# Cross-attention with a routed expert layer: expert weights kept on chip and copied by register, the last group routed like all others, sets of 9, 4 and 3 groups

## The chip, the cores and the metric

The kernel runs on one core of a Trainium2 chip. The metric is the time of one execution on the device in microseconds (us); lower is better. The core has a tensor engine (PE; its weight loads are listed as PEld), a vector engine (DVE), a scalar engine (ACT), a GpSimd engine (POOL) and SyncE (SP), which here only issues transfers. Each engine works through its own instructions in order, and semaphores tie the engines together.

## The reference

64 sequences of 128 tokens, 128 features each. First cross-attention to a context of 77 rows, then a mixture of 8 experts of which each token takes two, and a shared expert for all tokens:

```
x = x + xattn(layernorm(x), ctx)          # 16 heads of 64, softmax, output projection, bias
x2 = layernorm(x); logits = x2 @ router_w.T
idx = top_k(softmax(logits), 2)           # gate[t, e] = logits[t, e] for the two chosen, else 0
for e in range(8):
    h = silu(x2 @ w1[e].T) * (x2 @ w3[e].T)          # 176 hidden
    moe += gate[:, e:e+1] * (h @ w2[e].T)
moe += (silu(x2 @ sw1.T) * (x2 @ sw3.T)) @ sw2.T     # shared expert
x = x + moe
```

Everything is float32.

## The kernel before

**Groups, units, steps.** The 64 sequences are 16 groups of 4 (`G`), 512 tokens each. Attention runs over 128 units (one sequence, half of the heads); a hand-written plan (`at(step, ...)`) hangs all other work on 256 steps, two for each unit, so 16 for each group. Each engine's order is the order in which the program is written out: a last loop ties every instruction to the one before it on its engine.

**Routing.** While group g+1 is in attention, a `Router` normalises group g, transposes it, computes the logits (L514), chooses two experts for each token (`choose`, `choose_second`, small DVE operations), and in `place` (L554 to L599) counts with PE and DVE which row of a DRAM buffer each token goes to. `send` (L604) scatters the rows with 8 indirect DMAs that POOL issues, one for each sequence and choice. The shared expert follows, and `park` (L633) writes the sum to DRAM.

**Sets and blocks.** Groups are collected in sets (`SETS`, 7, 5 and 3). When a set's last group is placed, `tables` (L692) makes on DVE the table of blocks: which 128 rows belong to which expert. A `Quad` is four blocks of 128 rows; sets of 7, 5 and 3 groups have 16, 12 and 8 quads, always worked in full. `Quad.load` (L748) reads from the tables into SP registers and has SP issue, for each block, one DMA for its rows (`xb`, L757) and one for its expert's weights (`w`, L765, 312 KB from DRAM). Then `transpose` (PE L771, ACT L773), `first` and `rest` (PE L778, ACT tanh L465 and L477, DVE L467 to L482), `down` (PE L790 and L791, the destination rows `to` on DVE L793, the scaling `y` on ACT L798) and `answer`: four indirect DMAs on POOL (L802), which scatter the results to DRAM. `Combine` reads a group's parked rows (L821) and its answers (L822, 512 KB), adds them on DVE (L829, two additions) and has SP store the result (L833).

**What runs where.** The quads of the first two sets are spread over attention steps. Their p (the step of `transpose`) goes from `st.ready` to shortly before the next set is ready: 16 quads over steps 127 to 203, 12 over 207 to 251.

**The ending.** After attention, `ending` works through 17 jobs in an order of its own: the 8 quads of the last set, the shared expert of the last group, and the last group itself, which is not routed: class `Dense` passes all its 512 tokens through each of the 8 experts (PE L655, L669, L670) and adds each result with the gate as a factor (DVE L672). Quads and dense jobs alternate; the last three jobs are dense. In iteration k the program writes `first` of job k, `transpose` of job k+1, `rest` of job k, then `down` and `answer` of job k-1. The five combines of the set before the last and the three of the last set have their transfers issued by POOL; their additions are written two iterations behind their loads. Buffers: `y` has 2, `xb` 4, the weights `w` 12, `ya` 3.

**Last values.** `values_of_last` (L424) takes its staging tile from the same single buffer ("c") as the comparisons of `tables`.

Of the kernel before, what the change touches and what calls it, by code (L numbers as in the profile page):

```python
# [31 lines left out]
G = 4  # L32
NG = B // G

SETS = (7, 5, 3)
# [13 lines left out]
NHR = 3  # L49
# [3 lines left out]
NOWHERE = 1e6  # L53
# [5 lines left out]
def xattn_moe_kernel(  # L59
# [32 lines left out]
    def weights_of(engine, w, q, n, name):  # L92

        to = ffn.tile([128, WALL], F32, tag="w", name=f"{name}_{q}", bufs=3 * QUAD)
        to = to[:, : 4 * n].rearrange("p (m d) -> p m d", d=n)
        engine.dma_start(out=to, in_=w[:, 4 * q : 4 * (q + 1), :])
        return to
# [40 lines left out]
    wsh_sb = const.tile([128, WALL], F32, name="wsh_sb")  # L138
    nc.scalar.dma_start(out=bo_sb, in_=b_out.rearrange("(o d) -> o d", o=1).broadcast_to([128, D]))
    nc.sync.dma_start(out=rw_sb, in_=rwT)  # L140
    nc.sync.dma_start(out=wsh_sb, in_=wsh)

# [25 lines left out]
    dest = const.tile([128, most, 2 * G], F32, name="dest")  # L168
    spare = const.tile([128, nb], F32, name="spare")
# [8 lines left out]
    def more_constants():  # L178
        for e in range(E):
            nc.gpsimd.memset(rank[:, :, e : e + 1], float(E - e))  # L180
        nc.gpsimd.memset(upto, 0.0)
        for e in range(E):
            nc.gpsimd.memset(upto[:, e, : e + 1], 1.0)
            nc.gpsimd.memset(first_row[:, e : e + 1], float(e * rows))
        iota(block_no, [[1, nb]], 0, 0)
        iota(block_row, [[128, nb]], 0, 0)
        nc.gpsimd.memset(ones, 1.0)
        nc.gpsimd.affine_select(before, ones, [[1, 128]], ALU.is_gt, 0.0, base=0, channel_multiplier=-1)
        iota(dest, [[2 * T, most], [1, 2 * G]], 0, 2 * G)
        iota(spare, [[128, nb]], most * 2 * T, 1)  # L190
        for h in hrs:
            nc.gpsimd.memset(h, 0.0)
        nc.gpsimd.memset(nobody, 0.0)
        nc.gpsimd.memset(nobody[:, D : D + 1], NOWHERE)
        for to in sent:
            nc.sync.dma_start(out=to[E * rows :, :], in_=nobody)
# [99 lines left out]
    class Attention:  # L296
# [15 lines left out]
        def keys(self, p, i):  # L312

            if i == 0:
                self.kx[p] = grp.tile([D, NH, KP], F32, tag="kx", name=f"kx_{self.g}_{p}")
# [169 lines left out]
    class Router:  # L485


        def __init__(self, g, st, x1):
            self.g, self.st, self.x1 = g, st, x1
            self.j = g - st.start if st else None  # L490
# [63 lines left out]
        def place(self):  # L554
# [24 lines left out]
            for src, to, by in ((at, pos, 1.0), (self.lg, self.pay[:, :, :, D + 1].rearrange("p c b -> p c b"), 0.5)):  # L579
# [9 lines left out]
            nc.vector.tensor_copy(  # L589
                self.pay[:, :, :, D], dest[:, j, :].rearrange("p (c b) -> p c b", c=2)  # L590
# [44 lines left out]
    class Dense(Router):  # L635


        def __init__(self, g, st, x1):
            super().__init__(g, st, x1)
            self.w, self.he, self.hre = {}, {}, {}  # L640

        def gates(self):

            sel = self.t3("place")
            nc.vector.tensor_tensor(sel, self.oh[:, 0], self.oh[:, 1], ALU.add)
            self.gate = self.t3("grest")
            nc.vector.scalar_tensor_tensor(self.gate, self.lg, 0.5, sel, ALU.mult, ALU.mult)

        def load(self, e):
            self.w[e] = ffn.tile([128, WALL], F32, tag="w", name=f"w_d{e}", bufs=3 * QUAD)  # L650
            nc.sync.dma_start(out=self.w[e], in_=wx[e * 128 : (e + 1) * 128, :])

        def up_of(self, e):
            def up(to, c, m):
                nc.tensor.matmul(to[:m], self.w[e][:, c : c + m], self.x2T, start=True, stop=True)  # L655

            return up

        def first(self, e):
            self.he[e] = gated(f"d{e}", self.up_of(e))  # L660

        def rest(self, e):
            self.hre[e] = gated_rest(f"d{e}", self.up_of(e))

        def down(self, e):
            py = bank(f"pd_{e}")
            for b in range(G):
                ts = slice(b * NQ, (b + 1) * NQ)
                nc.tensor.matmul(py[:, ts], self.he[e][:, ts], self.w[e][:, W2F:W2R], start=True, stop=False)  # L669
                nc.tensor.matmul(py[:, ts], self.hre[e][:, ts], self.w[e][:, W2R:], start=False, stop=True)  # L670
            for b in range(G):
                nc.vector.scalar_tensor_tensor(  # L672
                    self.x1[:, b, :],
                    py[:, b * NQ : (b + 1) * NQ],
                    self.gate[:, b, e : e + 1],
                    self.x1[:, b, :],
                    ALU.mult,
                    ALU.add,
                )
                if e == E - 1:  # L680
                    nc.sync.dma_start(out=out[self.g * G + b], in_=self.x1[:, b, :])

    def values(a, most):
        return nc.values_load_multi_w_load_instructions(
            a,
            engines=[mybir.EngineType.SP],
# [5 lines left out]
    def tables(st):  # L692
# [47 lines left out]
        nc.vector.tensor_scalar(st.w_row, ex, float(E - 1), 128.0, ALU.min, ALU.mult)  # L740

    class Quad:
# [5 lines left out]
        def load(self):  # L748
            st = self.st
            self.w = []  # L750
            self.xb = ffn.tile([128, QUAD, DW], F32, tag="xb", name=f"xb_{self.name}", bufs=4)
            first = slice(QUAD * self.q, QUAD * (self.q + 1))
            froms = values(st.from_row[0:1, first], E * rows)
            wrows = values(st.w_row[0:1, first], (E - 1) * 128)
            for j in range(QUAD):
                w = ffn.tile([128, WALL], F32, tag="w", name=f"w_{self.name}_{j}", bufs=3 * QUAD)
# [8 lines left out]
                nc.sync.dma_start(out=w, in_=wx[bass.ds(wrows[j], 128), :])  # L765
                self.w.append(w)
# [19 lines left out]
        def down(self):  # L786
            py = bank(f"pq_{self.name}")
            for j in range(QUAD):
# [5 lines left out]
                self.to, self.xb[:, :, D], spare[:, QUAD * self.q : QUAD * (self.q + 1)], ALU.min  # L794
# [17 lines left out]
    class Combine:  # L812
# [5 lines left out]
        def load(self):  # L818
# [5 lines left out]
                in_=answers[st.i][j * 2 * T : (j + 1) * 2 * T, :].rearrange("(p k) d -> p k d", p=128),  # L824
# [75 lines left out]
    def route(g, step, *args):  # L900
        if g not in routers:
            st = next((s for s in sets if s.start <= g < s.start + s.n), None)
            routers[g] = (Router if st else Dense)(g, st, atts[g].x1)
# [10 lines left out]
    assert g == NG - 1  # L914
# [3 lines left out]
    for st in sets:  # L918
        for g in range(st.start, st.start + st.n):
            p = 16 * (g + 1)  # L920
            routing(g, p, (7, "place"), (11, "shared_up"), (12, "shared_rest"), (14, "shared_down"), (17, "park"))
            for k in range(4):
                for c in range(2):
                    at(p + 8 + k, lambda g=g, c=c, b=k: routers[g].send(c, b))
        at(p + 9, lambda st=st: tables(st))

        st.ready = p + 15
    end = 16 * NG

    for st, after in zip(sets, sets[1:]):  # L930
        until = after.ready - 4
        for q in range(st.quads):
            quad = Quad(st, q)
            p = st.ready + (until - st.ready) * q // (st.quads - 1)
            at(p - 3, quad.load)
            at(p, quad.transpose)
# [12 lines left out]
    class Job:  # L949


        def __init__(self, of=None, **steps):
            self.steps = {k: getattr(of, k) for k in ("load", "transpose", "first", "rest", "down") if hasattr(of, k)}
            self.steps.update(steps)
            if of is not None:
                self.steps["answer"] = lambda: [of.answer(j) for j in range(QUAD)]

        def do(self, step):
            self.steps.get(step, lambda: None)()

    def last(step, *args):
        return lambda: route(NG - 1, step, *args)

    before_last, last_set = sets[-2:]
    blocks = [Job(Quad(last_set, q)) for q in range(last_set.quads)]
    experts = [
        Job(load=last("load", e), first=last("first", e), rest=last("rest", e), down=last("down", e)) for e in range(E)
    ]
    shared = Job(first=last("shared_up"), rest=last("shared_rest"), down=last("shared_down"))
    jobs = blocks[:3] + [shared]  # L970
    for q, e in zip(blocks[3:], experts):
        jobs += [q, e]
    jobs += experts[len(blocks) - 3 :]

    ahead_of = {0: ["stats"], 1: ["normed"], 2: ["transpose", "logits"], 3: ["choose"], 4: ["choose_second", "gates"]}

    def finish(c, k):

        for n, step in ((0, c.load), (2, c.add), (2, c.store)):
            combining.setdefault(k + n, []).append(step)  # L980

    combining = {}
    for j in range(before_last.n):
        finish(Combine(before_last, j, nc.gpsimd), 2 + j)
    done = jobs.index(blocks[-1])
    for j in range(last_set.n):
        finish(Combine(last_set, j, nc.gpsimd), done + 2 + j)

    def ending():
        for k in range(max(len(jobs) + 2, max(combining) + 1)):  # L990
            job = jobs[k] if k < len(jobs) else Job()
            for step in ahead_of.get(k, ()):
                route(NG - 1, step)
            if k + 2 < len(jobs):
                jobs[k + 2].do("load")
            for step in combining.get(k, ()):
                step()
            job.do("first")
            if k + 1 < len(jobs):
                jobs[k + 1].do("transpose")  # L1000
            job.do("rest")
            if 0 < k <= len(jobs):
                jobs[k - 1].do("down")
                jobs[k - 1].do("answer")

    at(end - 3, lambda: jobs[0].do("load"))
    at(end - 2, lambda: jobs[1].do("load"))
    at(end - 1, lambda: jobs[0].do("transpose"))
# [132 lines left out]
```

## Time and profile before

| | |
|---|---|
| time, three runs | 1002.66 us median (1001.15 to 1005.33) |
| the profiled execution | 1007.26 us, of which 1005.6 us are the span from its first to its last instruction |
| busy share of the span | PE 96%, DVE 68%, ACT 61%, POOL 51% |
| granted PE clock, mean | 0.98 |
| DMA queues | 130.6 MB, mean 130 GB/s |
| weights `w` from DRAM | 144 loads of 312 KB for blocks, 8 for the dense jobs |
| indirect DMAs on POOL | 120 of `send`, 144 of `answer` |

Times within the profile are microseconds from the span's start, single durations often in nanoseconds (ns). A line of a timeline has the start, the duration, the engine, the source line, the operation, the written and read tiles, a count, and in brackets how long the engine had been idle and what ended that. A line of the windows view has, for a stretch of time, the busy time of PE, PEld, DVE, ACT and POOL with the number of instructions, then the granted clock, the share of the DMA engines and GB/s. A line of the chain of waits has the start, the duration and what the end of the program then depended on.

### The profile page before, as it was taken

The page shows a single profiled execution, that of the slowest core. Times are in us where ns is not written, and L with a number is a line of the kernel's source. Part 1 is how long each engine was busy: PE and PEld are TensorE (multiplying, and loading weights), DVE is VectorE, ACT ScalarE, POOL GpSimd, SP SyncE. Part 2 cuts the span into 40 slices and gives each one's busy share as a digit, 9 for nine tenths or more (in the row PEclk, how much of TensorE's full clock was granted, in tenths as well). Part 3 has the DMA queues.
Part 4 walks back from the last instruction along what each step waited for, and adds up shares of the span by engine and source line. Part 5 has one row for each costly group of instructions (what it writes and reads, how often), then busy time and mean ns, then how long its engine had stood idle before and what let it go on. Part 6 is the DMA issues. An engine that isn't in the chain of part 4 may idle for free.

```text
span 1005.6 us, 19274 instructions
## 1 busy us (share of the span) xinstructions
PE 960.8 (96%) x6219; PEld 791.8 (79%) x6219; DVE 682.9 (68%) x1758; ACT 612.9 (61%) x1345; POOL 512.9 (51%) x693
## 2 busy tenths in 40 slices
PE   7999999999999989999999999999999899898896
PEld 5887877777778858888788888887878788787684
DVE  4566776676666765857567666687668856665876
ACT  4776767666766655566666676665756656544341
POOL 3245363645455442574645648465465474663532
PEclk9999999999999999999999999999999999898997
DMA  5222112212211125544533454336568653267954
GB/s 174 69 63 74 45 43 74 74 31 64 71 57 58 56 85 162 159 133 129 172 117 105 129 178 144 106 112 195 187 205 266 213 161 119 71 193 230 340 183 147
DMA packets 100165, 130.62 MB, mean 130 GB/s; under 512 B 13408, under 2 KB 64352, under 8 KB 100064
## 3 DMA queue, kind: packets, MB, share of 16 engines
q1 hardware_dynamic: 84496, 96.27, 32.0%
q0 software_dynamic: 10240, 23.73, 6.8%
q10 hardware_dynamic: 5328, 9.37, 2.5%
q8 instruction: 50, 0.82, 0.4%
q14 instruction: 51, 0.42, 0.2%
HBM read 93.59 MB, written 35.74 MB: 129 GB/s over the span
## 4 chain that ended last, share of the span: by engine, by line
PE 75%; DVE 10%; ACT 7%; DMA 3%; issue 3%; POOL 1%; SPq 1%; DVEq 0%; ACTq 0%; POOLq 0%
PE py L415 13%; PE ps L336 11%; PE pk L319 10%; PE pv L388 8%; PE p L778 6%; PE pa L405 6%; PE pq L790 3%; PE pq L791 3%; PE p_s L615 2%; PE pn L425 2%; PE ph L778 2%; ACT pay L276 2%; ACT vo L393 1%; DVE sm L358 1%; PE pf L628 1%
## 5 line engine op out<-in xcount | busy, mean ns | idle before, releaser
L319 PEld LDWEIGHTS pk<-cT,wkq_sb 96*128 96x128 f32 x1024 | 158.2, 189 | 69.5 <-issue 45.2
L326 ACT COPY kx<-pk 128x308 f32<-128x308 f32 x256 | 105.2, 416 | 157.4 <-PE pk L319 152.3
L802 POOL DMA_INDIRECT answers<-y,to x144 | 141.2, 981 | 104.6 <-ACT y L798 47.1
L319 PE MATMUL pk<-cT,wkq_sb 96*128 96x154 f32 x1024 | 175.1, 294 | 0.7 <-DVE wkq_sb L237 0.7
L336 PE MATMUL ps<-kx,xgT 128*128 128x308 f32 x512 | 158.7, 431 | 5.3 <-DVE sc L347 5.3
L415 PEld LDWEIGHTS py<-vo,aT 128*128 128x128 f32 x1280 | 154.6, 194 | 11.2 <-ACT vo L393 1.8
L415 PE MATMUL py<-vo,aT 128*128 128x128 f32 x1280 | 155.2, 277 | 1.6 <-ACT vo L393 1.6
L604 POOL DMA_INDIRECT sent<-pay,row x120 | 118.3, 986 | 61.6 <-DVE part L594 30.7
L393 ACT COPY vo<-pv 64x512 f32<-64x512 f32 x256 | 147.2, 575 | 2.1 <-ACT vn L433 0.4
L368 POOL TENSOR_TENSOR at<-sc,ri 128x512 f32<-128x512 f32 x64 | 67.4, 1053 | 154.8 <-DVE ri L360 118.2
L351 ACT ACTIVATE sc<-sc,rs_a 128x616 f32<-128x616 f32 x128 | 104.9, 819 | 50.5 <-DVE sc L347 41.0
L358 DVE TENSOR_REDUCE sm<-sc 128x8 f32<-128x616 f32 x128 | 101.2, 790 | 44.9 <-ACT sc L351 44.1
L388 PE MATMUL pv<-wvo_sb,cM 96*128 96x512 f32 x256 | 131.0, 593 | 0.2 <-DVE x L416 0.2
L366 POOL TENSOR_TENSOR at<-sc,ri 128x256 f32<-128x256 f32 x128 | 76.2, 618 | 104.4 <-DVE ri L360 53.1
L408 ACT COPY aT<-pa 128x512 f32<-128x512 f32 (+1 forms) x256 | 96.4, 430 | 42.5 <-PE pa L405 35.7
L336 PEld LDWEIGHTS ps<-kx,xgT 128*128 128x128 f32 x512 | 89.1, 191 | 30.2 <-DVE sc L347 6.0
L345 DVE TENSOR_REDUCE mx<-ps 128x8 f32<-128x616 f32 x128 | 98.7, 771 | 19.7 <-PE ps L336 18.4
L347 DVE TENSOR_TENSOR sc<-ps,mx 128x616 f32<-128x616 f32 x128 | 102.4, 800 | 12.9 <-DVE mx L345 1.0
L405 PE MATMUL pa<-ident,at 128*128 128x128 f32 x640 | 90.9, 272 | 0.0
L405 PEld LDWEIGHTS pa<-ident,at 128*128 128x128 f32 x640 | 75.7, 141 | 12.7 <-issue 12.3
L778 PEld LDWEIGHTS p<-xT,w 128*128 128x128 f32 x576 | 69.7, 196 | 7.1 <-issue 3.4
L778 PE MATMUL p<-xT,w 128*128 128x128 f32 x576 | 72.8, 280 | 1.9 <-ACT xT L773 1.7
(155 smaller groups left out, 1461.8 us busy)
## 6 DMA issues: line engine op xcount, KB each, us to landing
w<-in_wx_dram SPq DMA_DIRECT2D x144, 312.0 KB, 4.1
xb<-sent SPq DMA_DIRECT2D x144, 65.0 KB, 3.5
last_values<-vn ACTq DMA_DIRECT2D x32, 256.0 KB, 2.4
vo<-last_values SPq DMA_DIRECT2D x64, 128.0 KB, 3.4
xg<-in_x_dram SPq DMA_DIRECT2D x16, 256.0 KB, 3.0
xgT<-in_xT_dram SPq DMA_DIRECT2D x16, 256.0 KB, 2.6
ya<-answers POOLq DMA_DIRECT2D x8, 512.0 KB, 4.8
parked<-x SPq DMA_DIRECT2D x15, 256.0 KB, 2.7
```

The source lines that it names most:

```text
L319: nc.tensor.matmul(pk[:, k].rearrange("p (b k) -> p b k", k=NKV), wkq_sb[:, 2 * i + k, :], self.cT[:, 2 * p : 2 * (p + 1), :], start=True, ...
L326: nc.scalar.copy(self.kx[p][:, hs, :], pk)
L336: nc.tensor.matmul(ps[:, r, : 4 * NKV].rearrange("p (j k) -> p j k", k=NKV), self.xgT[:, ts], self.kx[p][:, h : h + 4, ks], start=True, st ...
L351: nc.scalar.activation(at, at, AF.Exp, scale=self.norm.rs[:, b : b + 1])
L358: nc.vector.tensor_reduce(sm, at, AX.X, ALU.add)
L388: nc.tensor.matmul(pv, self.cM[:, p, KM * r : KM * (r + 2)], wvo_sb[:, h : h + 4, :], start=True, stop=True)
L393: nc.scalar.copy(self.vo[b][rows, 4 * t : 4 * (t + 1), :], pv[rows].rearrange("p (m d) -> p m d", d=D))
L405: nc.tensor.transpose(pa[:, j * NQ : (j + 1) * NQ], keys[:, c : c + 128], ident)
L415: nc.tensor.matmul(py[:, :D], aT[:, m, :], vo[:, m, :], start=(m == 0), stop=(m == NT - 1))
L604: ins = nc.gpsimd.indirect_dma_start(out=sent[st.i], out_offset=bass.IndirectOffsetOnAxis(ap=self.row[:, i : i + 1], axis=0), in_=self.pay ...
L778: nc.tensor.matmul(to[:m, ts], self.w[j][:, c : c + m], self.xT[:, ts], start=True, stop=True)
L802: ins = nc.gpsimd.indirect_dma_start(out=answers[st.i], out_offset=bass.IndirectOffsetOnAxis(ap=self.to[:, j : j + 1], axis=0), in_=self.y ...
```

## The change

All eight experts' weights are loaded once into one tile `wx_sb` (SP, one load for each of groups 2 to 9). `Quad.load` now loads rows alone; a new step `Quad.weights` copies the four blocks' weights from `wx_sb` to working tiles: ACT and DVE each read two expert numbers into registers and do two copies of 128x624. `Dense` is gone: the last group is placed, sent and given to its experts through the last set, which has 3 groups as before; the sets have 9, 4 and 3 groups, so 20, 10 and 8 quads. Of the second set's 10 quads, 3 run beside attention (steps 223 to 246) and 7 (`KEPT`) in the ending, ahead of the last set. The first set's 20 quads run at steps 159 to 219, its nine combines after them. Room is made by fewer buffers (`w` 8, `hr` 2) and by putting the weights of every second pair of jobs of the ending into the attention's key tiles. The answers' buffer has its spare rows first (`block_row` with `max` in place of `spare` with `min`).

```diff
-SETS = (7, 5, 3)
+SETS = (9, 4, 3)
+KEPT = 7
-NHR = 3
+NHR = 2
+    def load_expert(e):
+        nc.sync.dma_start(out=wx_sb[:, e, :], in_=wx[e * 128 : (e + 1) * 128, :])
...
-                nc.sync.dma_start(out=w, in_=wx[bass.ds(wrows[j], 128), :])
+        def weights(self, room=None):
+            self.w = []
+            half = QUAD // 2
+            for k, (engine, copy) in enumerate(
+                ((mybir.EngineType.Activation, nc.scalar.copy), (mybir.EngineType.DVE, nc.vector.tensor_copy))
+            ):
+                first = QUAD * self.q + half * k
+                for j, e in enumerate(values(self.st.w_row[0:1, first : first + half], E - 1, engine)):
+                    if room is None:
+                        w = ffn.tile([128, WALL], F32, tag="w", name=f"w_{self.name}_{half * k + j}", bufs=2 * QUAD)
+                    else:
+                        w = room[:, (half * k + j) * WALL : (half * k + j + 1) * WALL]
+                    copy(w, wx_sb[:, bass.ds(e, 1), :].rearrange("p o w -> p (o w)"))
+                    self.w.append(w)
...
+    kept = []
     for st, after in zip(sets, sets[1:]):
+        quads = [Quad(st, q) for q in range(st.quads)]
+        until = after.ready - 4 if after is not sets[-1] else end - 10
+        if after is sets[-1]:
+            quads, kept = quads[:-KEPT], quads[-KEPT:]
+        for q, quad in enumerate(quads):
+            p = st.ready + (until - st.ready) * q // (len(quads) - 1)
             at(p - 3, quad.load)
+            at(p - 1, quad.weights)
...
+    jobs = blocks[:KEPT] + [shared] + blocks[KEPT:]
+    ahead_of = {
+        0: [last("stats"), last("normed")],
+        1: [last("transpose"), last("logits")],
+        2: [last("choose"), last("choose_second")],
+        3: [last("place")],
+        4: [last("send", c, b) for b in range(G) for c in range(2)],
+        5: [lambda: tables(last_set)],
+    }
+    def combine(st, k, queue):
+        for j in range(st.n):
+            c = Combine(st, j, queue)
+            for n, step in ((0, c.load), (1, c.add), (1, c.store)):
+                ahead_of.setdefault(k + j + n, []).append(step)
+    combine(before_last, KEPT + 2, nc.gpsimd)
+    combine(last_set, len(jobs) + 1, nc.sync)
     def ending():
...
+        for k in range(max(ahead_of) + 1):
+            for step in ahead_of.get(k, ()):
+                step()
+            do(k + 2, "load")
+            do(k, "first")
+            do(k + 1, "transpose")
+            do(k + 1, "weights")
+            do(k, "rest")
+            do(k - 1, "down")
+            do(k - 1, "answer")
```

## The prediction

> **What bounds the kernel now.** I read the windows view first, by stage: attention without quads, the crowded last groups before the end of attention, and the ending (from the last attention addition, L416 at 901.3, to the end).
>
> ```profile
> 53.00:327.00 274.00, 271.34 (x1650) 214.73 (x1650) 187.80 (x539) 188.34 (x403) 136.87 (x186) 1.00 0.18 58
> ...
> 688.00:824.00 136.00, 130.80 (x893) 112.61 (x893) 96.89 (x235) 84.10 (x189) 75.46 (x93) 0.97 0.69 214
> ...
> 901.30:1005.60 104.30, 88.14 (x558) 71.68 (x557) 73.31 (x156) 35.44 (x80) 43.48 (x52) 0.90 0.70 226
> ```
>
> Attention is PE's: 99% busy at full clock, 45.7 us a group. In the ending PE is busy for 88 of 104 us, at clock 0.90. What PE needs for one job of the ending is in the chain of waits, in a stretch without stalls:
>
> ```profile
> 952.30 1.79 PE p L778 x16
> 954.09 0.87 PE ph L778 x8
> ...
> 956.75 1.72 PE p_d L655 x4
> 958.47 0.43 PE pt L771 x4
> 958.90 0.86 PE ph_d L655 x2
> 960.21 0.22 PE pq L790 x2
> ...
> 961.55 1.79 PE p L778 x16
> ```
>
> From 952.30 to 961.55 is one quad and one dense job: 9.25. By parts a quad is 1.79 + 0.87 + 0.43 + 8 x 0.22 = 4.85, a dense job 1.72 + 0.86 + 8 x 0.22 = 4.34, together 9.2.
>
> The third view is POOL's timeline in the ending, since every quad ends in four indirect DMAs there.
>
> ```profile
> 972.01 0.96 POOL L802 DMA_INDIRECT answers<-y,to  x1 [4.50 <-ACT y L798]
> 973.28 0.96 POOL L802 DMA_INDIRECT answers<-y,to  x1 [0.30 <-issue]
> 974.54 0.96 POOL L802 DMA_INDIRECT answers<-y,to  x1 [0.30 <-issue]
> 975.80 0.96 POOL L802 DMA_INDIRECT answers<-y,to  x1 [0.30 <-issue]
> 980.82 0.96 POOL L802 DMA_INDIRECT answers<-y,to  x1 [4.05 <-ACT y L798]
> ...
> 984.61 0.95 POOL L802 DMA_INDIRECT answers<-y,to  x1 [0.30 <-issue]
> 985.55 0.58 POOL L821 DMA_DIRECT2D ya<-parked  x1
> 987.13 0.57 POOL L822 DMA_DIRECT2D ya<-answers  x1 [1.00 <-DMA answers<-y,to]
> ```
>
> Starts are 1.264 apart: 0.96 of work and 0.30 that nothing shortens. Four are 5.06, more than PE's 4.85 for a quad. It costs nothing today, because a dense job, which needs no POOL, follows each quad: POOL waits 4 us for the next `y`.
>
> **Work removed and moved, on PE.** 36 quads and 8 dense jobs become 38 quads: 2 x 4.85 - 8 x 4.34 = -25 us of PE. The place matters more. Beside attention run 28 quads now and 23 (20 + 3) after. That stage is PE's, so 5 x 4.85 = -24.3.
>
> **Crowding.** 20 quads fall on steps 159 to 219, 5.3 a group (now 3.4, later 4.4). By DVE, ACT and POOL there is room, but the losses are already visible: against 45.7 for a group and 4.85 a quad, the five groups from 380 to 688 (16 quads; 308 us) lose 2.0 in all, the two from there to 824 (8 quads; 136 us) 2.9 each. Their gaps look like this one, PE waiting for DVE's choice, then 3.4 us at half clock:
>
> ```profile
> 732.63 0.18 PE L561 MATMUL pr<-sel,before 128*128 128x32 bf16 x1 [2.44 <-DVE sel L558]
> ```
>
> After: 4.75 groups (the crowded ones and group 14 with nine combines) at 2.9 = 13.8, against 2.0 + 5.8 = 7.8 now: +6. The bounds are 0, if the losses stay as they are, and +16, if four groups each open one more gap of 2.4 with its 1.7 of lost clock. The stall of `tables` (7 us at 371, DVE waiting for the staging tile, then half clock) keeps its count: now at groups 7 and 15, after at 9 and 13.
>
> **The copies.** No row has such a copy. Nearest on ACT is the 128x512 copy `pay` (627 ns; 112 columns more at the slope from 128 to 512 columns of L408 make 0.72); on DVE the 128x616 subtraction L347 (800 ns) is the upper end, the small copies (189 ns) the lower. I take 0.72 and 0.8, plus a register read of 0.3 (299 ns on SP, 1.3 at most). A quad gives ACT 2.92 + 1.44 + 0.3 = 4.7 and DVE 2.9 + 1.6 + 0.3 = 4.8, both under POOL's 5.06; beside attention ACT comes to some 80%. Covered by PE or POOL they cost nothing of their own; if that cover is gone, up to 0.7 a quad. The Trainium skill (VectorE: DVE Perf Modes, The perf-mode tier table) runs a float32 copy within SBUF at twice the rate; by its 58 + 624/2 cycles a DVE copy would be an estimated 0.39.
>
> **Transfers removed.** 152 loads of 312 KB go, 8 come. No PE gap beside attention names them. In the ending they stand in the chain with 3.6% of the last 165 us (6 us), but that stretch is rebuilt anyway: the kept quads' rows are long there, and the ending should start without a stall.
>
> **The ending after.** 15 quads and the shared job: PE 15 x 4.85 + 4.34 = 77. POOL: 60 answers + 8 sends of the last group = 68 x 1.264 = 86.0, and 8 transfers of combines at 0.57 = 4.6; POOL is now the longer queue. Step by step from the last attention addition:
> - first answer at +10: 1 for the first job's matmuls, 9.0 from its tanh to its answers (971.85 to 980.82 in a quad now);
> - POOL's 90.6, and 1.9 waiting for the second set's last answers to land before their combine is read (1.85 in the chain now);
> - a loop: additions are now written one iteration behind their load, ahead of the DVE work of that job, and the destinations `to` of the job before stand behind both. From POOL's transfer: 0.57 to issue, 4.9 to land (median 4.8 to 5.0), 1.4 for the additions, then u, h, two copies, ur, hr and to, 4.3: the next answers start 11.2 later, while POOL needs 7.4 for what stands between. Every second of the four rounds loses 3.8: +7.6;
> - 1.6 for the last answers to land (985.56 to 987.13 now): 10 + 90.6 + 1.9 + 7.6 + 1.6 = 111.7;
> - the last set's three combines come one behind the other, because on SP the store of one stands ahead of the loads of the next. The nearest row is the kernel's own SP combines:
>
> ```profile
> 770.47 0.39 SPq L833 DMA_DIRECT2D out_dram<-ya  x1
> 770.96 0.45 SPq L821 DMA_DIRECT2D ya<-parked  x1
> 771.46 0.44 SPq L822 DMA_DIRECT2D ya<-answers  x1
> ...
> 778.19 0.40 SPq L833 DMA_DIRECT2D out_dram<-ya  x1
> ```
>
> 7.7 a round, the shortest of six. So 6.8 for the first (0.5 + 4.9 + 1.4), 2 x 7.7, and 3.4 from the last store to the end (1002.21 to 1005.6 now): 25.6. The ending is 137.3 against 104.3 now: +33. The last group's chain (norm, logits, choice, place, 8 sends, `tables`, rows of the first quad) lies beside the seven kept quads: POOL should finish the sends near +35, the rows land near +45, the job that needs them comes near +48. Bare, each us there would be one.
>
> **One rule against the change.** The longest indirect DMAs now lie beside DVE additions with both inputs in SBUF (the first at 940.72 for 1.42):
>
> ```profile
> 941.85 1.14 POOL L802 DMA_INDIRECT answers<-y,to  x1 [0.30 <-issue]
> ```
>
> 1.14 against 0.96; over eleven such meetings the mean surplus is 0.12 us. For the 30 new DVE copies of the ending that is 0 to 4; I take 0 and keep the other end. The Trainium skill (SBUF — State Buffer, Who interferes with whom) says that a float32 copy within SBUF takes the port pair that DVE and GpSimd share for its whole duration, and that GpSimd cannot write descriptors meanwhile. By that, 30 x 0.39 would add an estimated 12 to POOL's queue, and more beside attention; no row here shows it.
>
> **The sum.** -24.3 + 6 + 33 = +14.7 on the profiled execution (1007.26, so 1022). That one stands 4.6 above the median 1002.66; on the median the sum gives 1017.4, I say 1017. A change under 0.5% (5 us) could not be told from none here.
>
> **The rivals.**
> 1. *POOL binds as above* (0.5): 1017. Bounds: crowding 0 to +16, port 0 to +4, the loop 0 to +7.6: from 1017 - 6 - 7.6 = 1004 to 1017 + 10 + 4 = 1031.
> 2. *Transfers get short without the weights* (0.2): the DMA share of the ending is 0.70 now. If the combines' loads land in 3.0 as the 256 KB loads do, the loop loses 1.9 twice (3.8 less), the tail 3 x 1.9 = 5.7 less, and crowding costs nothing (6 less): 1002, no change. Against: the landings of 4.8 to 5.0 are for twice the bytes.
> 3. *The ending runs at PE's pace* (0.15; faster): indirect DMAs one behind the other start closer than 1.264, or enough of POOL's queue falls into the time when only the shared job runs. Then 10 + 15 x 4.85 + 5.1 + 1.6 + 25.6 = 115 and no crowding: -24.3 + 10.7 = -13.6: 989. It decides where the mean pitch falls under (77 - 4.6) / 68 = 1.06. Against: the shortest pitch of some 150 is 1.258.
> 4. *Copies and POOL block each other* (0.15): DVE's copies hold POOL's descriptors up, or wait for them, by 0.8 each: 30 x 0.8 = 24 more in the ending: 1041.
>
> That the weights' transfers would not go is no rival: the changed program's order of instructions has the register reads and copies on ACT and DVE, and no such load on SP.
>
> **How the numbers follow.** Case 1 is the likeliest: 1017. The range leaves out most of case 3 and half of case 4: 996 to 1033. Faster by over 0.5% (under 997.6): case 3 and a rest of the others, 0.18. Within 0.5%: most of case 2 and the low end of case 1, 0.19. Slower: 0.63.
>
> **What would show it.** Right: the last attention addition near 883; in the ending POOL's answers back to back at 1.264 with PE gaps between, POOL's indirect DMAs ending some 110 us after attention; three SP rounds of 7 to 8 us with PE idle at the end; 25 us from the last answers to the end. Wrong: POOL waiting for `y` by several us a job as now, answers longer than 1.0, PE gaps in the crowded groups that name ACT or DVE copies, the last attention addition above 890, or a wait of the first quad of the last set for its rows.

## The result, and the profile after

The changed kernel takes 1034.24 us (median of 4, 1031.35 to 1035.67) beside 1004.0 for the kernel before: 1.0295 times as long (95% interval 1.0251 to 1.0339). 1017 was predicted, with a range up to 1033: the direction was right, the size 17 us too small. The profiled execution took 1035.67, 1033.9 of them in its span.

The windows view of the changed kernel, by the same stages (columns as before: stretch; busy PE, PEld, DVE, ACT, POOL; granted clock, DMA share, GB/s):

```profile
53.00:327.00 274.00, 271.33 (x1650) 214.70 (x1649) 187.78 (x540) 188.45 (x403) 136.83 (x186) 1.00 0.21 64
688.00:824.00 136.00, 130.06 (x883) 109.82 (x883) 99.29 (x253) 91.77 (x203) 78.49 (x95) 0.99 0.33 99
...
885.60:1033.90 148.30, 94.47 (x696) 87.06 (x695) 79.69 (x177) 62.51 (x141) 73.37 (x77) 0.82 0.38 109
```

Attention without quads is as it was. Attention ends at 885.6 in place of 901.3, so 15.7 us are won there. The ending takes 148.3 in place of 104.3, so 44 are lost. The weights' transfers are gone (DMA share 0.38, it was 0.70 in the ending), and POOL has risen from 43.5 to 73.4 us busy; with the 0.30 behind each of its 68 indirect DMAs that is 94.

The last attention addition on DVE, then POOL's timeline in the ending (in brackets the idle time before an instruction and what ended it):

```profile
885.63 0.29 DVE L425 TENSOR_TENSOR x<-py,x 128x128 f32<-128x128 f32 x1 [1.62 <-PE py L424]
...
904.27 1.04 POOL L773 DMA_INDIRECT answers<-y,to  x1 [15.96 <-ACT a L474]
...
911.76 0.96 POOL L773 DMA_INDIRECT answers<-y,to  x1 [2.66 <-issue]
...
915.88 1.03 POOL L773 DMA_INDIRECT answers<-y,to  x1 [0.63 <-issue]
...
952.06 0.96 POOL L773 DMA_INDIRECT answers<-y,to  x1 [0.30 <-issue]
953.01 0.61 POOL L792 DMA_DIRECT2D ya<-parked  x1
955.24 0.57 POOL L793 DMA_DIRECT2D ya<-answers  x1 [1.62 <-DVE to L764]
...
961.53 0.58 POOL L793 DMA_DIRECT2D ya<-answers  x1
966.13 1.02 POOL L773 DMA_INDIRECT answers<-y,to  x1 [4.02 <-ACT a L474]
...
971.85 0.58 POOL L793 DMA_DIRECT2D ya<-answers  x1
973.95 1.02 POOL L773 DMA_INDIRECT answers<-y,to  x1 [1.52 <-ACT a L474]
...
979.46 0.77 POOL L793 DMA_DIRECT2D ya<-answers  x1
982.91 1.01 POOL L773 DMA_INDIRECT answers<-y,to  x1 [2.68 <-issue]
...
990.79 0.96 POOL L773 DMA_INDIRECT answers<-y,to  x1 [2.66 <-issue]
...
996.33 0.96 POOL L773 DMA_INDIRECT answers<-y,to  x1 [0.48 <-ACT a L474]
...
1010.21 0.96 POOL L773 DMA_INDIRECT answers<-y,to  x1 [0.30 <-issue]
```

From 915.9 to 953 and from 996 to 1011 POOL issues one indirect DMA every 1.26 us or little more, as predicted: it is the longer queue. But its first answer comes 18.6 us after the last attention addition, and between the two full stretches it idles once for landing answers (1.62) and five times more (4.02, 1.52, 2.68, 2.66 and 0.48). The last lines of the tail, from SP and DVE:

```profile
1017.44 0.39 SPq L804 DMA_DIRECT2D out_dram<-ya  x1
...
1023.98 0.39 SPq L804 DMA_DIRECT2D out_dram<-ya  x1
...
1029.12 1.42 DVE L800 TENSOR_TENSOR ya<-ya 128x512 f32<-128x512 f32 x2 [5.17 <-DMA ya<-answers]
1030.57 0.39 SPq L804 DMA_DIRECT2D out_dram<-ya  x1
```

Three rounds one behind the other, 6.5 and 6.6 apart, with PE idle.

### The profile page after: what moved, and what is told of

The parts are those of the page before. It is cut to its first block, busy times and chain, and to the rows that moved or that the text cites. A ratio compares the mean times of both kernels' runs of the same rounds, so it can differ in the third digit from the quotient of the medians.

```text
span 1033.9 us, 18911 instructions
## 1 busy us (share of the span) xinstructions
PE 944.4 (91%) x6136; PEld 781.0 (76%) x6136; DVE 692.2 (67%) x1792; ACT 655.6 (63%) x1419; POOL 528.5 (51%) x699
## 5 line engine op out<-in xcount | busy, mean ns | idle before, releaser
L773 POOL DMA_INDIRECT answers<-y,to x152 | 150.3, 989 | 100.1 <-ACT a L474 28.1
L424 PEld LDWEIGHTS py<-vo,aT 128*128 128x128 f32 x1280 | 155.8, 195 | 11.2 <-issue 1.3
L613 POOL DMA_INDIRECT sent<-pay,row x128 | 127.9, 999 | 64.9 <-DVE part L603 31.9
L749 PE MATMUL p<-xT,w 128*128 128x128 f32 x608 | 84.5, 294 | 10.9 <-DVE w L736 9.7
L749 PEld LDWEIGHTS p<-xT,w 128*128 128x128 f32 x608 | 78.8, 207 | 14.7 <-DVE w L736 10.7
```

Of the source, the lines that this page charges most:

```text
L424: nc.tensor.matmul(py[:, :D], aT[:, m, :], vo[:, m, :], start=(m == 0), stop=(m == NT - 1))
L613: ins = nc.gpsimd.indirect_dma_start(out=sent[st.i], out_offset=bass.IndirectOffsetOnAxis(ap=self.row[:, i : i + 1], axis=0), in_=self.pay ...
L749: nc.tensor.matmul(to[:m, ts], self.w[j][:, c : c + m], self.xT[:, ts], start=True, stop=True)
L773: ins = nc.gpsimd.indirect_dma_start(out=answers[st.i], out_offset=bass.IndirectOffsetOnAxis(ap=self.to[:, j : j + 1], axis=0), in_=self.y ...
```

## The experiments

Theory A: the loss is the ending of the routed last group, in which POOL's fixed pitch is the longer queue, with three separate losses on top: the late first answer, the additions of the combines, the tail in single file. Theory B: the copies of the weights cost what is lost. Later theories stand with their runs.

All ratios are to the kernel before on the same chip. The chips differ. Those of the first result and of the run with the routing one iteration later take 1004 to 1008 for the kernel before, the others 1045 to 1052. There the profile shows a place beside attention where PE's signals stay out for up to 10 us and no wait of the program explains it. The ratio of the changed kernel is the same on both sorts (1.0295; 1.026 and 1.0303). But single stages are longer there, so a stage's microseconds are compared with the changed kernel's on such a chip: 169.5 and 166.2 in its ending. The runs from the two halves to the tail, the additions two iterations behind, the plain transfers, the routing steps behind rest and the first run of the three repairs share the chip of the 169.5. The second run of the three repairs and the last row share the chip of the 166.2. "Only the stores moved", "three repairs, plain transfers" and "work shared out anew" ran on a third of the slower chips, without the changed or the repaired kernel beside them, so for these only ratios from other chips can be compared.

One difference matters below: between the first answer and the last POOL idles 16.3 us in the changed kernel on the first chip (idles over 0.35), and 39.8 on the chip of the 169.5. The traces from the slower chips also hold some 30% fewer semaphore updates (11790 for 16429 in the changed kernel), so there the name of what ended a wait is less sure than its length.

| kernel | ratio to before (95%) | last attention addition | ending |
|---|---|---|---|
| changed kernel, one of the slower chips | 1.026 (1.0195 to 1.0325) | 910.3 | 169.5 |
| changed kernel, another of the slower chips | 1.0303 (1.0255 to 1.0351) | 912.2 | 166.2 |
| before, weights on chip with copies | 1.0018 (0.999 to 1.0047) | 950.5 | 105.3 |
| changed, weights from DRAM, no copies | 1.0305 (1.0253 to 1.0357) | 913.0 | 175.8 |
| tail together | 1.0185 (1.0145 to 1.0225) | 910.1 | 160.9 |
| additions two iterations behind | 1.0161 (1.0123 to 1.02) | 908.0 | 158.3 |
| only the stores moved | 1.0259 (1.0201 to 1.0317) | 905.5 | 167.7 |
| plain transfers for answers | 0.9857 (0.9799 to 0.9915) | 909.1 | 128.4 |
| routing steps behind rest | 1.0246 (1.0186 to 1.0307) | 909.2 | 164.2 |
| three repairs | 1.0107 (1.0061 to 1.0153) | 911.0 | 148.0 |
| three repairs, again | 1.0098 (1.0065 to 1.0131) | 907.9 | 145.9 |
| three repairs, plain transfers | 0.9773 (0.9718 to 0.9829) | 908.7 | 117.8 |
| three repairs, work shared out anew | 1.0106 (1.0049 to 1.0162) | 921.1 | 144.2 |
| three repairs, routing one iteration later | 1.0202 (1.0158 to 1.0246) | 884.9 | 140.4 |
| the same, routing behind the answers too | 1.0215 (1.0181 to 1.0249) | 907.4 | 153.9 |

**The two halves of the change apart.** First the copies alone, in the kernel before with its sets and its dense last group; then the routed last group alone, in the changed kernel with the weights loaded by SP.

```diff
 # in the kernel before
+            at(p - 1, quad.weights)          # copies from wx_sb by ACT and DVE
-                nc.sync.dma_start(out=w, in_=wx[bass.ds(wrows[j], 128), :])
 # in the changed kernel
-            at(p - 1, quad.weights)
+                nc.sync.dma_start(out=w, in_=wx[bass.ds(wrows[j], 128), :])
```

> The kernel before with one half of the change alone: weights on chip, copied by ACT and DVE for each quad; the dense jobs read theirs in place; sets 7, 5, 3 and the dense last group stay. Theory A (the loss comes from routing the last group, that is from POOL's queue, the routing chain at the head of the ending and the combines behind it): not slower than before; the two stalls of the ending for rows and weights (899 to 910 and 941 to 948) shrink, the crowded groups lose no more than now: 990 to 1004. Rival B (the copies on ACT and DVE, with their register reads, cost the time): slower, 36 quads at 0.8 or more: 1020 to 1035.

> The changed kernel with the other half alone: last group routed, sets 9, 4, 3, seven quads kept for the ending, but each block's weights loaded from DRAM by SP as before, no copies. Theory A: as slow as the changed kernel or a little slower, 1030 to 1045, with the same gaps of PE at the head of the ending, POOL's answers back to back, and the same tail. Rival B: back near the kernel before or faster, 1000 to 1012, since the copies are gone.

Copies in place of loads, with all else as before, change nothing that can be measured (1.0018). The routed last group without copies loses as much as the whole change (1.0305). Theory B falls as the cause of the loss. So does the hope that copies in place of transfers win time: 46 MB less through the queues (84.6 in place of 130.6), and no time.

The second run does not show that the copies are free within the changed kernel's ending, for there the loads take their place and cost time of their own. POOL's answers are not back to back, as had been expected: PE waits 35.5 us in 25 places for rows (`xb`), which SP issues in turn with the weights; in the changed kernel on the same chip it waits 1.8 us for them. And the first answer comes 15.5 us after the last attention addition, not 18.7.

**The tail.**

```diff
-                ahead_of.setdefault(k + j + n, []).append(step)
+                ahead_of.setdefault(k + j * apart + n, []).append(step)
-    combine(last_set, len(jobs) + 1, nc.sync)
+    combine(last_set, len(jobs) + 1, nc.sync, 0)      # apart = 0: three loads, then the rest
```

> The changed kernel, but the loads of the last set's three combines are all issued before the first of their additions and stores. Theory A: the two later rounds of 6.6 us fall together with the first; the three loads (2.3 MB) land within some 8 us of the last answers: 7 to 9 us less than the changed kernel, 1025 to 1028. Rival (the transfers share one bandwidth and one latency anyway): 0 to 3 us less, 1031 to 1035.

The ratio falls from 1.026 to 1.0185, and from the end of the last indirect DMA to the end of the program it takes 15.5 in place of 22.6: the rounds in single file were a loss of their own.

**The additions, and which queue they hold up.**

```diff
 # additions two iterations behind
-            for n, step in ((0, c.load), (1, c.add), (1, c.store)):
+            for n, step in ((0, c.load), (behind, c.add), (behind, c.store)):   # behind = 2
 # only the stores moved
-            for n, step in ((0, c.load), (1, c.add), (1, c.store)):
+            for n, step in ((0, c.load), (1, c.add)):
...
             do(k + 2, "load")
+            for step in stores.get(k, ()):
+                step()
```

> The changed kernel, but the four combines of the second set have additions and stores two iterations behind their loads in place of one. Theory A: DVE no longer waits for the loads in front of a job (4.3, 1.8, 2.9 and 1.9 us now) and POOL's idle times after its transfers (4.0, 1.5, 2.7 and 2.7) go: 5 to 9 us less, 1025 to 1030. Rival (POOL waits there for the first quads of the last set to come through PE, not for the additions): the same, 1033 to 1036.

> Of the second set's four combines only the stores move: in each iteration they are written behind the loads of the rows of the quad two jobs on, instead of ahead of them; the additions stay where the change put them. Theory S: what costs time in that stretch is SP's queue, in which a store that waits for the additions stands ahead of the rows of the next quad (in the chain of the changed kernel: additions at 960.0, store, rows landed at 967.3, PE waiting for them); then this edit alone wins most of what two iterations of distance won, 7 to 13 us or 0.7 to 1.2% of the changed kernel, and no PE gap names xb there. Theory D, the one of the prediction: the additions on DVE stand ahead of the next quad's own DVE work; then under 3 us (0.3%) is won.

Two iterations of distance win about 1% (1.0161 against 1.026). The second run was made because the chain of waits of the changed kernel passes from the additions (959.24 to 960.7) through SP's store to the rows of the next quad (962.27 to 967.3). Moving the stores alone gives 1.0259, beside 1.026 and 1.0303 for the changed kernel on other chips: at most 0.4%, where theory S expected 0.7% or more. The trace agrees with theory D: with the stores moved PE still waits 5.9 and 5.4 us (at 1006.8 and 1025.0) for weight copies on DVE that stand behind the additions, and no gap over 1 us names `xb`; with additions two iterations behind, no such gap is left. So theory S falls, and the additions on DVE, one iteration behind their load, are what holds the ending up. A chain names one path; here another, through DVE, lay beside it.

**POOL's price.**

```diff
+            if st.i:                                  # sets 2 and 3
+                if j == QUAD - 1:                     # one a quad, in block order
...
+                    ins = nc.gpsimd.dma_start(
+                        out=answers[st.i][r0 : r0 + QUAD * 128, :].rearrange("(j p) d -> p j d", p=128), in_=self.y
+                    )
...
+                return
             ins = nc.gpsimd.indirect_dma_start(       # set 1: four a quad
```

> In the last two sets the four scattering transfers of a quad become one plain transfer of POOL of the same bytes, written in block order (the rows are not put where the tokens belong, so the output is another; all else is as in the changed kernel). Theory A, POOL's fixed pitch of 1.264 us carries the middle of the ending: 60 answers (75.8 us) become 15 transfers of at most 1 us, POOL waits for y before each of them, and the ending shrinks from 148 to PE's pace: 18.6 to the first answer, 14 x 4.85 + 4.34 for the jobs behind it, the gaps of some 15 us that PE has now, 21 for the tail: 127, so about 20 us or 2% less than the changed kernel. Theory C, the ending is held by the chain of additions, destinations and weight copies on DVE, and POOL only stands behind it: PE's gaps stay, less than 8 us (0.8%) is won.

The ending falls to 128.4; theory A had put it at 127. That the total is so near is luck, since the 127 was added up from the first chip's numbers and two errors cancel: from the first answer to the last it takes 94.7 us, not 87, and behind the last 15.1, not 21. From the changed kernel on that chip, 169.5, the fall is 41 us, twice what was expected, because there its ending was 21 us longer than on the first. Of these 41, 33.5 lie between the first answer and the last (128.2 before). The other 7.5 lie behind them and are not the pitch: a plain transfer writes rows that the program knows, and the answers for the first of the last set's combines are read at 1009.32, ahead of the last transfer at 1021.60; the scattering transfers leave all three behind the last answers. POOL now waits for each quad:

```profile
1014.94 0.75 POOL L777 DMA_DIRECT2D answers<-y  x1 [6.04 <-ACT y L769]
```

0.76 a quad (median) in place of 4 x 1.264. Theory C falls: the additions' and copies' waits alone do not hold the ending.

**The lead, and all repairs together.**

```diff
-        0: [last("stats"), last("normed")],
-        1: [last("transpose"), last("logits")],
-        2: [last("choose"), last("choose_second")],
-        3: [last("place")],
-        4: [last("send", c, b) for b in range(G) for c in range(2)],
-        5: [lambda: tables(last_set)],
+        5: [last("send", c, b) for b in range(G) for c in range(2)],
+        6: [lambda: tables(last_set)],
+    }
+    behind = {
+        0: [last("stats"), last("normed")],
+        1: [last("transpose")],
+        2: [last("logits"), last("choose"), last("choose_second")],
+        3: [last("select")],
+        4: [last("place")],
...
             do(k, "rest")
+            for step in behind.get(k, ()):
+                step()
```

`select` is the first DVE step of `place` (`sel`), written one iteration ahead of the rest.

> The last group's routing steps stand behind the rest step of their iteration instead of at its head, its logits and its counts one step behind what they wait for, and its sends and table one iteration later. Theory A, these steps held the first answers back by 9 us because PE, DVE and ACT met them ahead of the kept jobs: the gaps of 2.8 and 4.2 us on PE's logits and counts go, the first answer comes at +10 to +12 after the last attention addition instead of +18.6, and the time falls by 6 to 10 us (0.6 to 1.0%) against the changed kernel, unless the later sends make the first quad of the last set wait for its rows (then a PE gap that names xb). Rival: POOL's queue is full from its first answer to its last and the chain of the last group only moves, so under 3 us is won.

> The three repairs together: routing steps behind the rest step, additions of the second set's combines two iterations behind their loads, the three loads of the last combines issued together. Theory A, three separate losses: their sum, some 8 + 10 + 11 us or 2.5 to 3% less than the changed kernel, so 0.995 to 1.007 of the kernel before: the ending is then POOL's 91 us with about 10 in front and 16 behind it, 116 to 120 against 104, and the attention stage gives the 15 back. Rival: the losses overlap, so the best single repair is nearly all there is to win: 1.2 to 1.6% less than the changed kernel, still 1.3% or more slower than before.

The first answer comes at +15.8 in place of +18.7, not at +10 to +12. 2.9 us of lead went with 3.2 of time (1075.86 against 1079.06), which fits one for one but is less than the spread of the changed kernel's runs (1074.75 to 1081.42). All three repairs together (this edit, the tail's and the additions'): 1.0107, and 1.0098 in a later run beside the changed kernel's 1.0303:

> The changed kernel itself, run beside the next three so that each can be set against it on one chip. Every theory expects about the first ratio to the kernel before, 1.0295 (1.025 to 1.034), and in its profile an ending some 43 us longer and an attention stage some 15 us shorter than before.

> The changed kernel itself beside the other two. 1.0295 (1.025 to 1.034) of the kernel before on the chip of its first runs, 1.026 on the second.

> The kernel with the three repairs once more (1.0107 of the kernel before, 1.5 to 1.8% less than the changed kernel, on another chip). Theory A, separate losses that add up: 1.5 to 2.5% less than the changed kernel here too. Rival: on a chip without the pauses of PE the repairs overlap: 1.2% or less.

So 1.5% and 2.0% less. The single repairs give 0.75, 1.0 and 0.15%, together 1.9%: within the noise they add up, but to less than the 2.5 to 3% that theory A expected, the lead above all.

**What remains.**

> The three repairs, and the answers of the last two sets written by one plain transfer for each quad (rows not put where the tokens belong, so another output). Theory A, what is left of the loss in the repaired kernel is POOL's queue of scattering transfers: the time goes from 1.011 of the kernel before to 0.96 to 0.98, and PE is busy from the first job to the last with gaps under 12 us in all. Rival, the plain transfers won only because they removed the waits that the repairs remove too: then it stays within 1% of the plain transfers without repairs (0.986), or is no better.

```diff
-KEPT = 7
+KEPT = 5
-    jobs = blocks[:KEPT] + [shared] + blocks[KEPT:]
+    jobs = blocks[:2] + [shared(NG - 3)] + blocks[2:4] + [shared(NG - 2)] + blocks[4:KEPT] + [shared(NG - 1)] + blocks[KEPT:]
```

> The three repairs, and work shared out anew between the stages: the shared expert of groups 13 and 14, which needs no POOL, moves into the ending, and two of the kept quads move beside attention (KEPT 5). If POOL alone carries the ending of the repaired kernel: attention gains 2 x 4.34 and gives 2 x 4.85 (+1 us), POOL's queue loses 8 x 1.264 (-10 us): 0.8 to 1.0% less than the repaired kernel, 1.000 to 1.004 of the kernel before. If PE and POOL are both full there (PE keeps 2 x 4.34 more and 2 x 4.85 less work, so the same): under 0.3% is won. Either way not clearly under the kernel before.

With plain transfers the repaired kernel falls by 3.3% to 0.9773, below the kernel before: what remains of the loss goes with the scattering transfers. Of the 30 us that the ending loses (148.0 to 117.8), 22 lie between the first answer and the last, which is POOL's queue; 8 lie behind, where again combines are loaded before the last answers. Sharing the work out anew wins nothing (1.0106): the ending is 4 us shorter (144.2 for 148.0), but attention ends 10 us later (921.1 for 911.0, and for 908.7 with plain transfers on its own chip) where 1 was expected, so neither theory had the size of that part. No version that computes the whole result beat the kernel before.

**Why the first answer is late.**

```diff
 # one iteration later; in the second run these steps also stand behind "answer"
-        0: [last("stats"), last("normed")],
+        1: [last("stats"), last("normed")],
...
-        6: [lambda: tables(last_set)],
+        7: [lambda: tables(last_set)],
...
+            if k == KEPT:
+                do(k + 1, "load")
+            if k != KEPT - 1:
+                do(k + 2, "load")
```

> The repaired kernel (all three repairs), with the last group's routing one iteration later still, so that nothing of it stands ahead of the first quad's answers; the rows of the first quad of the last set are loaded one iteration later in exchange. Theory L: the lead of 10 us from the last attention addition to the first answer was the right size for quads alone, and the routing steps in PE's, ACT's and DVE's queues made 15.8 and 18.6 of it: the first answer comes at +10 to +12. Rival: the lead was sized from a stretch with dense jobs between the quads and is too short for quads behind each other: it stays at +14 or more. The time is no test of these, since the rows come later: from 0.5% less to 0.7% more than the repaired kernel (1.011), with a PE gap that names xb.

> As the kernel with the routing one iteration later, but the routing steps also stand behind the answers of their iteration, so that ACT's pay no longer stands ahead of the first quad's scaling. Theory L: in the run before, the first quad's last matmul ended 9.2 us after the last attention addition and its scaling waited 5.5 us behind pay; without that the first answer comes at +10.5 to +12. Rival: another wait takes the place, and it stays at +14 or more. The time stays within 0.5% of that kernel (1.020), since the rows of the last set's first quad still come late.

The first of the two missed: +15.4. The steps were one iteration later but still ahead of the scaling `y`, which waited on ACT's queue behind `pay`. Put behind the answers, the first answer comes at +11.4 (907.4 to 918.77): theory L. ACT's timeline in that run has nothing but quads ahead of it (the last line is POOL's first answer):

```profile
915.81 0.59 ACT L486 ACTIVATE ar<-ph 48x512 f32<-48x512 f32 x1
916.59 1.14 ACT L775 ACTIVATE y<-pq,xb 128x128 f32<-128x128 f32 x4 [0.20 <-PE pq L768]
918.77 0.96 POOL L779 DMA_INDIRECT answers<-y,to  x1 [16.24 <-issue]
```

In the changed kernel the same stretch, ACT and PE:

```profile
888.55 1.65 ACT L285 ACTIVATE pay<-x,shift_f,rs_f 128x128 f32<-128x128 f32 x4 [4.46 <-DVE shift_f L283]
890.10 0.57 ACT L474 ACTIVATE a<-p 128x512 f32<-128x512 f32 x1
...
893.38 1.88 PE L523 MATMUL pl<-rw_sb,x2T_f 128*128 128x8 f32 x8 [2.81 <-ACT x2T_f L298]
895.12 3.76 PE L749 MATMUL p<-xT,w 128*128 128x128 f32 x16
```

The first job's tanh `a` waits behind `pay`, PE's logits wait 2.81 for `x2T`, and half clock follows (granted clock 0.50 from 893.4 to 898.8): the second job's `p` starts 9.5 after the last addition. In both kernels with the routing later it starts 3.6 after it and lasts 2.44 in place of 3.76:

```profile
888.51 2.44 PE L755 MATMUL p<-xT,w 128*128 128x128 f32 x16 [0.57 <-ACT w L742]
```

(from the first of the two, whose last attention addition is at 884.9). 5.9 + 1.3 = 7.2, the whole of 18.6 - 11.4. The copies have a part in it: two of them and their register read stand on ACT ahead of `x2T`, and in the run with the routing early but without copies the logits wait 1.6 in place of 2.8 and the first answer comes at +15.5. So some 3 of the 7.2 go away with either, the routing steps or the copies. In exchange both kernels load the last set's first rows late: PE waits 15.3 and 17.8 for them, and the time is worse than with three repairs (1066.76 against 1055.55 on one chip). Placed early, the steps cost 7 us of lead; placed late, they cost more.

## Why the prediction was right or wrong

- **The stage of attention: right.** 883 predicted, 885.6 measured. Quads still cost PE 4.9 each (`p` starts at 918.68 and 923.57 in the chain of the changed kernel's ending); the crowding took 8.6 in place of 6 (the remainder of the 15.7, with 4.85 a quad), inside its bounds.
- **POOL binds: right**, as the plain transfers show, and the pitch of 1.264 holds for runs of answers and sends. Between the first answer and the last POOL idles 16.3 of 106.9. Rival 3 (PE's pace) falls.
- **The first answer at +10: the step that failed.** 18.6, so 8.6 of the 17 us. The text said that the last group's chain "lies beside the seven kept quads" and looked only at when its sends and rows would be ready. Its ACT and PE steps, and with them weight copies that the sum called covered, stand ahead of the first quads in in-order queues, and at that moment POOL, the queue that sets the end, is empty. Without the routing steps the lead is 11.4, so the size for quads alone was 1.4 short. It had also been given no bounds, so the first case ended at 1031 and the range at 1033.
- **From the first answer to the last: 6.8 too short** (100.1 predicted, 106.9 measured). The loop was the right mechanism and had the right length: from a combine's transfer to the answers that its additions hold up it takes 10.9, 12.4, 11.1 and 11.3 (955.24 to 966.13, 961.53 to 973.95, 971.85 to 982.91, 979.46 to 990.79), for 11.2. On DVE the destinations `to` stand behind the additions and end 0.8 before the answers start:

```profile
959.24 1.47 DVE L800 TENSOR_TENSOR ya<-ya 128x512 f32<-128x512 f32 x2 [4.32 <-DMA ya<-answers]
...
965.20 0.16 DVE L764 TENSOR_TENSOR to<-xb,block_row 128x4 int32<-128x4 f32 x1
```

What was wrong is the count: the sum let every second of four rounds lose 3.8, and each of the four lost something. (Also, what stands between on POOL is 0.57 + 4 x 1.264 + 2 x 0.57 = 6.8 by its own rows, not 7.4.) With the 0.48 behind them the five idles come to 9.9 beyond 0.3 each, predicted 7.6. 2.7 more were lost at 911.76 and 915.88, where POOL waits for the second and third quad after the same routing steps. The landing wait was 0.6 shorter (1.3 beyond 0.3, for 1.9), and single DMAs longer than 0.96 (up to 1.37) make up most of the rest.
- **The tail: 4.4 too long** (22.8 from the last indirect DMA's end, 27.2 predicted). The answers of a combine landed in 3.4 to 4.1 without the weights' transfers, not 4.9. Here rival 2, which took 5.7 off the tail, had the better size; its loop and its crowding went the other way.
- **The median: 3.2.** The profiled execution of before stood 4.6 above its median, that of the changed kernel 1.4. 2.6 + 8.6 + 6.8 - 4.4 + 3.2 and 0.4 of rounding make the 17.
- **The copies: covered, as predicted, but at the head of the ending** (above).

```profile
L736 DVE COPY w<-wx_sb 128x624 f32 x76 | 36.6, 524 | 6.8 <-issue 5.4 <-DVE x L639 0.3
...
L736 ACT COPY w<-wx_sb 128x624 f32 x76 | 50.4, 712 | 3.9 <-issue 2.2 <-DVE mx L354 0.4
```

ACT's 0.71 was right (0.72). DVE's 0.52 (median 0.485) is nearer to the estimate of 0.39 from the Trainium skill (VectorE: DVE Perf Modes, The perf-mode tier table for the rate, The TRN2 errata for the cycles) than to the 0.8 that the sum took. Rival 4 falls. The skill's rule on the shared port (SBUF — State Buffer, Who interferes with whom) showed as a small surplus: the 27 indirect DMAs that lay over 0.1 us beside a DVE copy took 1.069 on average, the other 253 took 0.985. That is 2.3 us over the whole run, inside the bounds of 0 to 4 that the sum gave the ending alone, and far from the estimated 12.

## What to carry to other kernels

When work is moved onto the queue that will set the end, ask first when that queue gets its first item: each instruction that stands ahead of that item on any in-order engine delays it, however well the rest is covered; here that was 7 us, and moving the steps further back cost more than it won. Give every term of a sum its bounds, the small ones at the seams too. And price the engine that issues, not only the ones that compute: some 25 us of PE were to be saved here (its busy time fell from 960.8 to 944.4), and 60 answers at 1.264 us each, now without dense jobs between them, took more.

## What the runs showed of the hardware

- In no run do two of POOL's indirect DMAs start closer than 1.256 us; a plain transfer of four times the bytes took POOL 0.76.
- One load of register values took 0.49 us on ACT and 0.53 on DVE, 0.30 on SP (medians in the changed kernel).
- On the chips with the slower times the attention groups without quads run as on the others (46.9 and 44.7 us in turn from last addition to last addition), the first with quads some 9 us longer (82.9 and 82.5 for 73.8 in the changed kernel). In the profile of the first of these two ACT waits 9.65 us for a signal of PE there, and half clock follows (0.50 from 531.4 to 535). What causes it is open.
